# A two-layer spectral and convolution kernel: halves of the array in turn, pole planes loaded first, a second bank for the last batch

## The chip, the cores and the metric

The kernel runs on one core of one Trainium2 chip. A core has a matrix engine (TensorE, PE in the profile; PEld is its weight loading), a vector engine (VectorE, DVE), a scalar engine (ScalarE, ACT), a general engine (GpSimd, POOL) and an engine that only issues transfers here (SyncE, SP). Each runs its own instructions in their order, and they meet through semaphores. Transfers between device memory and the on-chip memory (SBUF) run on 16 DMA engines; SP and POOL each issue into a queue of their own. TensorE writes to PSUM, an accumulation memory[...]. The metric is the device time of the core, in microseconds (us).

## The reference

Input x is 16 batches x 16 channels x 256 x 256, float32. Two layers, each of the form x = x + layer(group_norm(x)), with 8 groups of 2 channels:

```
# layer 0: a Fourier layer with poles
alpha = fft2(gn(x))
A  = 1 / (omega1 - pole1);  Bm = 1 / (omega2 - pole2)      # 4 poles per axis and channel pair
S  = einsum('ikpq,oikp,xikq->oxik', residue, A, Bm)
out1 = einsum('biox,oxik->bkox', alpha, S)                 # mix of channels i -> k per frequency
out2 = einsum('bikpq,ikpq->bkpq', einsum(alpha, A, Bm), residue)
x = x + real(ifft2(out1)) + real(out2 x exponentials) / (256 * 256)

# layer 1: convolutions and a gate
f = mish(conv3x3(gn(x) per channel, 1 -> 4 features));  top, bot = halves of f's rows
ker = conv1x1(relu(conv1x1(bot)));  ti = sum over 9 taps of patches(top) * ker
out = mish(conv3x3(concat(ti, roll(bot)), 64 -> 16))
gate = sigmoid(3-tap conv over channels of mean(out));  x = x + gn(x) * gate
```

## The kernel before, in words

The kernel is four functions that run one after the other: `layer0_forward`, `layer0_mix`, `layer0_back` and `layer1`. What passes between them lies in device memory: `al` (spectrum), `hd` (mixed spectrum), `zn` (normalized input of layer 1), `cf` (features of layer 1), and tables `td`, `avd`, `ed`. In the forward the order of TensorE's instructions is the one written in the source, and a scheduler orders the other engines. In the other three functions PE, ACT, DVE and POOL all keep the order of the source. SP's transfers are ordered by the scheduler throughout. A tile pool with `bufs=n` gives n buffers to a tag in turn; a writer waits until the readers of the buffer's last tile are done.

**Forward.** 64 steps, one for each batch b and group of four channels (cg). A step loads x one step or two ahead (`fetch`, L162), computes the group norm's scalars with two tiny matmuls (gn_mean L34, gn_var L42) and DVE work between them (gnq L36 to L39), and forms the even and odd halves `eo`. `rows` multiplies by the Fourier table along y (pu, L207) and by the pole table (pv, L214), twice a step; ACT copies `right` (L222), DVE combines into `u` (L224), ACT writes `v` (L231). `poles` then computes `pd` (L241): for each of 2 pairs j of channels and 2 channels a of a pair, four accumulating products with 64 output columns, written to partitions 64a to 64a+63, so that channel a uses one half of the array. In the steps of every batch but the first, `columns` multiplies the batch before by the Fourier table along x (px, L313): for two frequency rows k of a tile, two halves h and two parts accumulate; row k is written to partitions 64k to 64k+63, again one half of the array. ACT moves px to `o` (L320), and POOL stores it to `al` (L329). The pool of px has two buffers. From step 4 on, DVE also computes tables, a piece a step (L415 to L534, L767 to L781). After the last step, `finish` and nine calls of `columns` do the last batch.

**Mix.** 33 groups g of four frequencies along y. `poles` (L618) multiplies the pole planes `av`, a 192 KB load of a group (L617), by a mask m8 into `lt` (L627, six DVE instructions); `residues` (L636) multiplies lt by the table `tt` into `s`: for each k, part v and half h one product to partitions 64h to 64h+63 (L641); DVE and ACT copy the products (L649, L651). `spread` copies the loaded spectrum `alc` into the operand `alb` (L598 on ACT, L600 on DVE). `mix` then multiplies s and alb (pg, L663), `turn` transposes, and `columns` transforms along x. Before the loop, SP's order is: ident, ix (1 MB), m8, four loads of tt (1 MB each), m4, eight loads of alc, then av of groups 0 and 1.

**Back** transforms along y, adds the poles' part and the input, and writes zn; the change doesn't touch it.

**Layer 1.** Units of rows (9 a batch) pass conv1 (L1027), mish (L1046, L1075), the reduction (L1054) and the involution (L1095, L1103, L1106), whose results go to cf. One batch behind, `conv2` (L1153) reads 17 row pairs for each of eight steps s (`rows`, L1155, 2176 KB, two buffers) and computes two halves q, each 24 accumulating products of 32 columns into one bank (c2ps, L1169), which ACT reads with mish and a running sum (e, L1178). c2ps has a pool of one bank (ps2); the pool psd with three banks serves the reduction, the involution and the gate's product. After a batch, `gate` (L1182) reduces the sums, forms a scale per channel, and in eight parts (four channels of half the rows) loads zn into `o` (L1193, four buffers), applies scale and mean on POOL (four instructions, L1216) and stores to the output (L1225). For the last batch no units are left: conv2's eight steps run alone, with the gate of the batch before beside them, and then its own gate ends the kernel.

Of the kernel before, what the change touches and what calls it, by code (L numbers as in the profile page):

```python
# [19 lines left out]
N = 256  # L20
G = 8
P = 128
# [50 lines left out]
def layer0_forward(ctx, tc, d, al, bd, tabs):  # L73
# [160 lines left out]
    def poles(cg, vts, acc):  # L234

        pd = psd.tile([P, 2, P], F32, tag="pd", name="pd")
        for j, vt in enumerate(vts):
            for a in range(2):
                ch = 4 * cg + 2 * j + a
                for n, (xh, k) in enumerate(((0, 0), (0, 1), (1, 0), (1, 1))):  # L240
                    nc.tensor.matmul(  # L241
                        pd[64 * a : 64 * a + 64, j],
                        lhsT=vt[:, a, xh, 64 * k : 64 * k + 64],
                        rhs=bt[:, xh, ch, 1 - k : 3 - k].rearrange("p l m -> p (l m)"),
                        start=n == 0,
                        stop=n == 3,
                    )
        gs = slice(2 * cg, 2 * cg + 2)

        def times(out, part, coef):  # L250
            shape = [P, 2, part.shape[2] // M, M]
            nc.vector.tensor_tensor(
                out.rearrange("p g (k q) -> p g k q", q=M),
                part.rearrange("p g (k q) -> p g k q", q=M),
                coef[:, gs].unsqueeze(2).to_broadcast(shape),
                ALU.mult,
            )

        t = dp.tile([P, 2, P], F32, tag="t", name="t")
# [42 lines left out]
    def columns(b, g0, rsc):  # L302

        u = us[b % 2]
        n = min(4, NF - g0)
        o = op.tile([P, 2, 2, N], F32, tag="o", name="o")
        for j in range(0, n, 2):
            lanes = 64 * min(2, n - j)
            ps = psx.tile([P, 2, 2, H], F32, tag="px", name="px")
            for k in range(min(2, n - j)):  # L310
                for h in range(2):
                    for part in range(2):
                        nc.tensor.matmul(  # L313
                            ps[64 * k : 64 * k + 64, :, h],
                            lhsT=u[:, h, part, g0 + j + k].rearrange("p f c -> p (f c)"),
                            rhs=wxn[:, h, part],
                            start=part == 0,
                            stop=part == 1,
                        )
            nc.scalar.activation(  # L320
                o[:lanes, j // 2],
                ps[:lanes].rearrange("p v h x -> p v (h x)"),
                AF.Copy,
                scale=rsc[:lanes],
            )
        for k in range(min(2, n)):
            w = (n - k + 1) // 2
            for v in range(2):
                nc.gpsimd.dma_start(  # L329
                    out=al[g0 + k : g0 + n : 2, v, :, b].rearrange("g p x -> p g x"),  # L330
                    in_=o[64 * k : 64 * k + 64, :w, v],
                )
# [221 lines left out]
def layer0_mix(ctx, tc, d, al, hd, tabs):  # L554
# [3 lines left out]
    nc = tc.nc  # L558
    nb = d["x"].shape[0]
    cp = ctx.enter_context(tc.tile_pool(name="mc", bufs=1))  # L560
    ident = load(nc, cp, d["ident"], [P, P], "ident")
    ix = load(nc, cp, d["ix"], [P, 8, N], "ix")
    m8 = load(nc, cp, d["m8"], [P, 8], "m8")

    tt = cp.tile([P, 2, C, N], F32, name="tt")
    for k in range(0, C, 4):
        nc.sync.dma_start(out=tt[:, :, k : k + 4], in_=tabs[0][:, :, k : k + 4])
    avd = tabs[1]

    alb = cp.tile([P, N, 4, nb], F32, name="alb")
    m4 = load(nc, cp, d["m4"], [P, 4], "m4")

    ap = ctx.enter_context(tc.tile_pool(name="ma", bufs=2))
    lp = ctx.enter_context(tc.tile_pool(name="ml", bufs=1))
    gp = ctx.enter_context(tc.tile_pool(name="mg", bufs=1))
    hp = ctx.enter_context(tc.tile_pool(name="mh", bufs=3))
# [31 lines left out]
    def spread(spectrum, f):  # L610
        for eng, parts in zip((nc.scalar, nc.vector), spreads[f]):
            for q, j in parts:
                expand(spectrum[q], q, j, eng)

    def load_poles(g):
        av = ap.tile([P, 32, 4, 3], F32, tag="av", name="av")
        nc.sync.dma_start(out=av.rearrange("p k f l -> p (k f l)"), in_=avd[g])  # L617
        return av  # L618

    def poles(av):  # L620

# [101 lines left out]
    E = mybir.EngineType  # L723
    with tc.manual_schedule(engines={E.PE, E.Activation, E.DVE, E.Pool}):
        spectrum = [load_spectrum(0, q) for q in range(4)]
        lt = poles(load_poles(0))
        av = load_poles(1)
        s = gp.tile([P, N, 2, C], F32, tag="s", name="s")
        for k0 in range(0, C, 2):
# [201 lines left out]
def layer1(ctx, tc, d, zn, cf, mr, nb):  # L931
# [225 lines left out]
    def conv2(b, s, acc):  # L1157
# [3 lines left out]

        begin = ((H + 1, 1, H + 2), (0, H + 1, 1))
        for q in range(2):
            ps = ps2.tile([P, 4, H], F32, tag="c2", name="c2ps")
            for blk in range(2):
                for dx in range(3):
                    x = begin[q][dx]
# [13 lines left out]
    def gate(b, acc):  # L1181
# [29 lines left out]
        for k in range(0, 8, 2):  # L1211
            following = [part(k + 2), part(k + 3)] if k < 6 else None
            c = k // 2 * 4
            for half, o in enumerate(parts):
                for i in range(4):
                    nc.gpsimd.tensor_scalar(  # L1216
                        o[:, i],
                        o[:, i],
                        scale[:, c + i : c + i + 1],
# [275 lines left out]
```

## Time and profile before

| what | value |
|---|---|
| median of 3 runs | 7388.45 us (7382.54 to 7390.2) |
| the profiled execution | 7392.98 us |
| its span, first to last instruction | 7391.2 us |
| PE busy | 6831.1 us (92%) |
| DVE busy | 4961.8 us (67%) |
| ACT busy | 3806.5 us (51%) |
| POOL busy | 3475.6 us (47%) |
| px, L313 | x4224, 557.8 us busy, 385 ns mean |
| pd, L241 | x2048, 164.3 us busy, 279 ns mean |
| c2ps, L1169 | x12288, 1395.3 us busy, 601 ns mean |
| gate's o, L1216 on POOL | x512, 280.5 us busy, 555 ns mean |

A profile is of one execution, taken on the chip. "Busy" is the time in which at least one instruction of a group runs; matmuls overlap, so busy time over count is less than the mean duration. The ends of matmuls are modelled. A fp32 matmul leaves two records, each with its weight load. In a timeline, a row merges instructions of one kind that follow each other: start, length, engine, line, operation, output<-input, partitions x elements, count, and in brackets the idle time before and what ended it. The forward runs from 0 to about 1408 us, the mix to about 2968, the back to about 3611, layer 1 to the end.

### The profile page before, as it was taken

The numbers are of one execution on the slowest core, as the hardware profiler recorded it, in microseconds if no ns is written. First come the engines' busy times: TensorE is split into PE (matmuls) and PEld (weight loads), VectorE is DVE, ScalarE is ACT, GpSimd is POOL, SyncE is SP. The second block draws the span as 40 slices with busy tenths as digits, with TensorE's granted clock in tenths as the row PEclk, the third lists the DMA queues.
The fourth block names the chain that finished last, engine by engine and source line by source line (L and its number), as shares of the span: only waits on it lengthen the run. The fifth ranks groups of instructions, "written<-read, shape, count | busy, mean of one in ns | idle before, by whom it ended". The sixth has DMA issues, their size and how long they took to land.

```text
span 7391.2 us, 147380 instructions
## 1 busy us (share of the span) xinstructions
PE 6831.1 (92%) x57640; PEld 3890.3 (53%) x57640; DVE 4961.8 (67%) x9441; ACT 3806.5 (51%) x5915; POOL 3475.6 (47%) x4636
## 2 busy tenths in 40 slices
PE   7889999799999999899789999999999999999996
PEld 5778888566666666677423333333333333333332
DVE  8999975366666666788676656665666666666662
ACT  2223333366666666222366656666666666656662
POOL 2334444322222222566554655555665565655554
PEclk9899999899999999999889999999999999999999
DMA  3444444333333332899767888888888888888886
GB/s 99 111 117 119 118 124 117 109 95 97 98 98 98 98 98 83 305 326 326 249 181 221 259 242 253 252 258 254 253 253 251 256 249 267 256 247 251 256 265 205
DMA packets 716089, 1443.59 MB, mean 195 GB/s; under 512 B 98954, under 2 KB 525254, under 8 KB 673638
## 3 DMA queue, kind: packets, MB, share of 16 engines
q1 hardware_dynamic: 567206, 959.76, 43.4%
q0 software_dynamic: 148192, 474.40, 20.6%
q8 instruction: 460, 7.54, 0.4%
q14 instruction: 231, 1.89, 0.1%
HBM read 877.12 MB, written 556.47 MB: 194 GB/s over the span
## 4 chain that ended last, share of the span: by engine, by line
PE 64%; DVE 7%; ACT 4%; issue 3%; DMA 2%; POOL 0%; SPq 0%; DVEq 0%; ACTq 0%; POOLq 0%
PE c2ps L1169 17%; PE c L1027 12%; PE pd L1095 12%; PE ph L698 5%; PE ps L641 5%; PE pg L663 4%; ACT wide L1075 3%; DVE alb L600 2%; PE pr L1054 2%; PE py L858 2%; PE py L859 2%; PE pt L679 1%; DVE zb L890 1%; DVE st L875 1%; DMA rows<-cf 1%
## 5 line engine op out<-in xcount | busy, mean ns | idle before, releaser
L1075 ACT ACTIVATE wide<-c,b 32x512 f32<-32x512 f32 x2176 | 1477.4, 679 | 354.6 <-PE c L1027 302.8
L1103 DVE TENSOR_TENSOR t<-pd,r 64x512 f32<-64x512 f32 x1088 | 744.3, 684 | 1295.9 <-PE pd L1095 1270.3
L1106 DVE TENSOR_TENSOR top<-pd,t 32x512 f32<-32x512 f32 x2176 | 1504.2, 691 | 52.6
L1169 PE MATMUL c2ps<-rows,c 128*32 128x512 f32 x12288 | 1395.3, 601 | 26.6 <-ACT e L1178 13.7
L1087 POOL COPY wide<-wide 32x1031 f32<-32x1031 f32 (+1 forms) x576 | 568.9, 988 | 1239.0 <-ACT wide L1075 1211.7
L1027 PE MATMUL c<-z,w 102*128 102x512 f32 x2048 | 1014.2, 628 | 138.5 <-ACT wide L1075 115.4
L1095 PE MATMUL pd<-wide,dw 128*128 128x512 f32 x2048 | 1012.5, 616 | 6.4 <-ACT r L1063 2.5
L1169 PEld LDWEIGHTS c2ps<-rows,c 128*32 128x32 f32 x12288 | 393.0, 109 | 993.6 <-issue 885.3
L718 POOL DMA_DIRECT2D hd<-h x512 | 323.5, 639 | 1227.6 <-DVE h L711 1203.5
L1027 PEld LDWEIGHTS c<-z,w 102*128 102x128 f32 x2048 | 401.2, 198 | 675.9 <-issue 486.0
L1095 PEld LDWEIGHTS pd<-wide,dw 128*128 128x128 f32 x2048 | 376.8, 194 | 614.3 <-issue 449.0
L1178 ACT ACTIVATE e<-c2ps,b 128x512 f32<-128x512 f32 x256 | 175.9, 687 | 845.6 <-PE c2ps L1169 842.9
L1088 POOL COPY wide<-wide 32x1031 f32<-32x1031 f32 (+1 forms) x576 | 572.2, 993 | 35.8
L313 PE MATMUL px<-wxn,u 128*64 128x256 f32 x4224 | 557.8, 385 | 2.2 <-ACT o L320 2.1
L641 PE MATMUL ps<-tt,lt 128*64 128x256 f32 x4224 | 495.5, 384 | 38.9 <-DVE lt L627 35.9
L698 PE MATMUL ph<-ix,yt 64*128 64x256 f32 x4128 | 502.5, 391 | 5.4 <-issue 4.7
L313 PEld LDWEIGHTS px<-wxn,u 128*64 128x64 f32 x4224 | 400.7, 136 | 127.0 <-ACT o L320 5.1
L698 PEld LDWEIGHTS ph<-ix,yt 64*128 64x128 f32 x4128 | 392.7, 190 | 91.7 <-issue 44.6
L1046 ACT ACTIVATE bot<-c,b 128x512 f32<-128x512 f32 x544 | 344.1, 684 | 175.7 <-PE c L1027 168.2
L207 PE MATMUL pu<-fy,eo 128*128 128x128 f32 x2048 | 425.5, 291 | 6.0 <-DVE u L224 4.4
L320 ACT ACTIVATE o<-px,rsc 128x512 f32<-128x512 f32 (+1 forms) x272 | 186.0, 686 | 472.2 <-PE px L313 441.1
L871 POOL TENSOR_TENSOR x<-x,o 128x512 f32<-128x512 f32 x256 | 324.0, 1266 | 216.7 <-DVE o L870 215.3
(203 smaller groups left out, 10818.5 us busy)
## 6 DMA issues: line engine op xcount, KB each, us to landing
rows<-cf SPq DMA_DIRECT2D x128, 2176.0 KB
z<-zn SPq DMA_DIRECT2D x768, 257.8 KB
cf<-top POOLq DMA_DIRECT2D x512, 240.0 KB, 7.1
cf<-bot POOLq DMA_DIRECT2D x96, 840.0 KB, 11.6
alc<-al SPq DMA_DIRECT2D x264, 256.0 KB
zn<-zb SPq DMA_DIRECT2D x128, 516.0 KB
o<-zn SPq DMA_DIRECT2D x128, 516.0 KB
z<-in_x SPq DMA_DIRECT2D x64, 1024.0 KB
```

The lines of the kernel that those rows point to most:

```text
L207: nc.tensor.matmul(pu[:, xh, e].rearrange("p v m -> p (v m)"), lhsT=lhs, rhs=fy[:, e], start=True, stop=True,)
L313: nc.tensor.matmul(ps[64 * k : 64 * k + 64, :, h], lhsT=u[:, h, part, g0 + j + k].rearrange("p f c -> p (f c)"), rhs=wxn[:, h, part], star ...
L641: nc.tensor.matmul(ps[64 * h : 64 * h + 64, v], lhsT=lt[:, h, k, 1 - v : 3 - v].rearrange("p l f c -> p (l f c)"), rhs=tt[:, h, k], start= ...
L698: nc.tensor.matmul(ph[q][:, e], lhsT=yt[lanes, i].rearrange("p t k -> p (t k)"), rhs=ix[lanes, i], start=n == 0, stop=n == 3,)
L1027: nc.tensor.matmul(ps[:, a], lhsT=w, rhs=z[:k, c : c + 2, 0:N], start=True, stop=True)
L1075: nc.scalar.activation(self.feat[64 - 32 * q : 96 - 32 * q, f, self.groups[g], :H], ps[q][32 * f : 32 * f + 32], AF.Mish, bias=b1[0][32 * ...
L1087: nc.gpsimd.tensor_copy(flat[0:32, f, 1:m], flat[64:96, f, 0 : m - 1])
L1088: nc.gpsimd.tensor_copy(flat[96:128, f, 0 : m - 1], flat[32:64, f, 1:m])
L1095: nc.tensor.matmul(ps, lhsT=dwt if self.tail else dw, rhs=self.feat[:, f, cs, :H], start=True, stop=True,)
L1103: nc.vector.tensor_tensor(t[64:128], ps[:64], self.r[:, cs], ALU.mult)
L1106: nc.vector.tensor_tensor(self.top[32 * f : 32 * f + 32, cs, q], ps[lanes], t[lanes], ALU.add)
L1169: nc.tensor.matmul(ps[32 * j : 32 * j + 32], lhsT=c2[:, blk, dx, :], rhs=t[:, 4 * j + blk : 4 * j + blk + 4, x : x + H], start=(blk, dx) = ...
```

## The change

Four edits. In the forward, `poles` issues the four accumulating products of two channels in turn, channel 0 and channel 1 alternating, instead of four of one and then four of the other; `columns` does the same with the two frequency rows k. The number of products and the tiles stay. In the mix, `load_poles` is defined earlier and the planes of group 0 are loaded right behind m8, ahead of tt; ident and ix follow tt. In layer 1, the second half q of every conv2 step of the last batch writes to a bank of psd instead of ps2. In the gate of the last batch, three of the four scaling instructions of a part go to DVE. Apart from these, each engine's instructions stand in the same order as before.

```diff
@@ layer0_forward.poles
         for j, vt in enumerate(vts):
-            for a in range(2):
-                ch = 4 * cg + 2 * j + a
-                for n, (xh, k) in enumerate(((0, 0), (0, 1), (1, 0), (1, 1))):
+            for n, (xh, k) in enumerate(((0, 0), (0, 1), (1, 0), (1, 1))):
+                for a in range(2):
+                    ch = 4 * cg + 2 * j + a
                     nc.tensor.matmul(
                         pd[64 * a : 64 * a + 64, j],
@@ layer0_forward.columns
-            for k in range(min(2, n - j)):
-                for h in range(2):
-                    for part in range(2):
+            for h in range(2):
+                for part in range(2):
+                    for k in range(min(2, n - j)):
                         nc.tensor.matmul(
                             ps[64 * k : 64 * k + 64, :, h],
@@ layer0_mix
-    ident = load(nc, cp, d["ident"], [P, P], "ident")
-    ix = load(nc, cp, d["ix"], [P, 8, N], "ix")
     m8 = load(nc, cp, d["m8"], [P, 8], "m8")
+    ap = ctx.enter_context(tc.tile_pool(name="ma", bufs=2))
+    avd = tabs[1]
+
+    def load_poles(g):
+        av = ap.tile([P, 32, 4, 3], F32, tag="av", name="av")
+        nc.sync.dma_start(out=av.rearrange("p k f l -> p (k f l)"), in_=avd[g])
+        return av
+
+    av = load_poles(0)
 
     tt = cp.tile([P, 2, C, N], F32, name="tt")
     for k in range(0, C, 4):
         nc.sync.dma_start(out=tt[:, :, k : k + 4], in_=tabs[0][:, :, k : k + 4])
-    avd = tabs[1]
+    ident = load(nc, cp, d["ident"], [P, P], "ident")
+    ix = load(nc, cp, d["ix"], [P, 8, N], "ix")
...
-        lt = poles(load_poles(0))
+        lt = poles(av)
         av = load_poles(1)
@@ layer1.conv2
         for q in range(2):
-            ps = ps2.tile([P, 4, H], F32, tag="c2", name="c2ps")
+
+            pool, tag = (psd, "d") if q and b == nb - 1 else (ps2, "c2")
+            ps = pool.tile([P, 4, H], F32, tag=tag, name="c2ps")
@@ layer1.gate
                 for i in range(4):
-                    nc.gpsimd.tensor_scalar(
+                    eng = nc.vector if i and b == nb - 1 else nc.gpsimd
+                    eng.tensor_scalar(
                         o[:, i],
                         o[:, i],
```

More of the change, by code (lines that the diff above doesn't have):

```diff
@@ L567, in layer0_mix @@
         nc.sync.dma_start(out=tt[:, :, k : k + 4], in_=tabs[0][:, :, k : k + 4])
-    avd = tabs[1]
+    ident = load(nc, cp, d["ident"], [P, P], "ident")
+    ix = load(nc, cp, d["ix"], [P, 8, N], "ix")
     alb = cp.tile([P, N, 4, nb], F32, name="alb")
     m4 = load(nc, cp, d["m4"], [P, 4], "m4")
-    ap = ctx.enter_context(tc.tile_pool(name="ma", bufs=2))
     lp = ctx.enter_context(tc.tile_pool(name="ml", bufs=1))
@@ L613, in spread @@
                 expand(spectrum[q], q, j, eng)
[L615 to L618, printed above, removed]
     def poles(av):
```

## The prediction

> **What bounds the kernel now.** I read the page first, then busy time by stretch, then waits and timelines of the places that the diff touches. The page's two rows, 185 us a slice:
>
> ```profile
> span 7391.2 us, 147380 instructions
> ...
> PE   7889999799999999899789999999999999999996
> ...
> DVE  8999975366666666788676656665666666666662
> ```
>
> TensorE (PE) is full nearly everywhere, so work taken off it should show, except in the first slices, where the vector engine (DVE) is as full. The forward stage ends at 1408 us (last px matmul). It has 64 steps, one per batch and channel group; a step runs from one start of pd to the next. Busy time in three stretches of it (columns: stretch, length, then busy us and count of PE, PEld, DVE, ACT, POOL; granted clock; DMA share; GB/s):
>
> ```profile
> 167.20:552.40 385.20, 338.65 (x2662) 296.15 (x2661) 353.90 (x1050) 104.82 (x194) 138.79 (x189) 0.91 0.41 113
> 552.40:1049.60 497.20, 490.51 (x4394) 422.59 (x4393) 457.43 (x1167) 188.53 (x333) 236.58 (x323) 1.00 0.45 122
> 1049.60:1362.90 313.30, 313.30 (x2866) 272.82 (x2865) 162.49 (x499) 96.25 (x191) 149.48 (x211) 1.00 0.40 105
> ```
>
> These are steps 5 to 19, 20 to 45 and 46 to 62. In the last, PE has no gap and DVE is half idle: PE alone binds. In the first, DVE builds tables and PE waits for it: the waits of that stretch give `PE gn_var L42 <- DVE gnq L39` 44.5 us in 15 waits, 3 us a step. The middle is shared. Its DVE waits:
>
> ```profile
> DVE arg L525 <- ACT n L523: 11.9, 12, 2.0
> DVE gnq L36 <- PE gn_mean L34: 9.6, 14, 1.6
> DVE arg L515 <- DMA ed<-arg: 6.5, 6, 1.5
> DVE st L174 <- DMA z<-in_x: 4.5, 6, 1.4
> ```
>
> One PE-bound step in the timeline (start, length, then what), and residue products of the mix, which already take the halves in turn:
>
> ```profile
> 1105.40 2.24 PE L241 MATMUL pd<-bt,v 128*64 128x128 f32 x29
> 1107.38 0.43 PE L313 MATMUL px<-wxn,u 128*64 128x256 f32 x1
> ...
> 1107.86 7.90 PE L313 MATMUL px<-wxn,u 128*64 128x256 f32 x62
> 1115.69 0.38 PE L34 MATMUL gn_mean<-mv,ones 128*128 128x2 f32 x2
> ```
>
> ```profile
> 2002.32 3.67 PE L641 MATMUL ps<-tt,lt 128*64 128x256 f32 x32
> 2005.92 0.92 PE L698 MATMUL ph<-ix,yt 64*128 64x256 f32 x6
> ```
>
> An fp32 matmul leaves two records. Forward: 32 pd and 64 px records take 1115.69 - 1105.40 = 10.29 us. Mix: 32 records of px's shape take 2005.92 - 2002.32 = 3.60 us, 112 ns each with the start; record starts inside are 216 ns apart per half, 108 overall. px also overlaps already (its starts come 920 ns per 8 records, 115 each, in mid-run, because a half's run of four overlaps the other's), but each burst begins and ends with one half alone.
>
> The mix's start:
>
> ```profile
> 1409.56 3.72 SPq L567 DMA_DIRECT2D tt<-td  x4
> ...
> 1430.80 14.40 SPq L617 DMA_DIRECT2D av<-avd  x3
> 1441.15 3.70 DVE L627 TENSOR_TENSOR lt<-av,m 128x512 f32<-128x512 f32 x6 [66.15 <-DMA av<-avd]
> ...
> 1444.91 5.43 PE L641 MATMUL ps<-tt,lt 128*64 128x256 f32 x34 [0.68 <-DVE lt L627]
> ```
>
> PE stands from 1408 to 1443 for 192 KB of pole planes that are queued behind 4 MB of tt, 1 MB of ix and 2 MB of alc. The end of layer 1:
>
> ```profile
> 7297.55 5.40 PE L1169 MATMUL c2ps<-rows,c 128*32 128x512 f32 x48 [0.95 <-ACT e L1178]
> ...
> 7317.70 5.44 PE L1169 MATMUL c2ps<-rows,c 128*32 128x512 f32 x48 [1.95 <-DMA rows<-cf]
> ```
>
> Each conv2 half waits some 0.95 us for ACT to empty the one bank; two of the later ones wait for rows instead.
>
> **What the Trainium skill says.** TensorEngine Tiling (Array Packing), Key Properties: "Different tiles can execute LdWeights and Matmul in parallel"; the 3.60 us above agree. TensorE: Matmul & The Clock Gate, Part 1: an idle window of some 3.4 us halves the PE clock; the mean of 0.91 where PE waits, 1.00 elsewhere, agrees. DMA: Bandwidth & Descriptors, Queues, rings and completion order: descriptors of one ring are taken in order; av, issued at 1430.80 behind alc and used at 1441.15, agrees. SBUF — State Buffer, Who interferes with whom: DVE's two-port tensor_scalar and GpSimd (POOL) block each other; no row of this trace shows it for the new tail.
>
> **Part 1, forward (pd and px by halves in turn).** Nothing is added; the same 96 records per step, in the same place of every queue. pd: full-width 128-column records start 109 ns apart (8 transposes pt take 1.09 us), so two halves in turn 54.5: 32 x 54.5 = 1.74. px: 64 x 108 = 6.91. Start 0.15 as in the mix. Sum 8.80 against 10.29: 1.49 saved a step (1.54 in one step of four, which has 8 px records more). A px tile then takes 1.73 us instead of 1.84; ACT empties it in 0.69 behind two buffers, so no new wait. By stretch:
> - steps 0 to 3, pd alone: some 0.5 each, 2.0. Step 4 (PE full in it): 1.5.
> - steps 5 to 19: PE's saved time is added to its 3 us wait for gnq, which stands behind table work on DVE. DVE's own waits there (24.6 us, u on right) follow gn_var and not px. 0.
> - steps 20 to 45: from below 0, from above 497.2 - 457.4 = 39.8 by DVE's busy time, or 26 x 1.49 = 38.7. DVE's waits for the sine on ACT (11.9) and for DMAs (6.5 + 4.5) are only partly PE's doing; if they stay, 457.4 + 22.9 = 480.3, 17 saved. I take 17.
> - steps 46 to 62: 17 x 1.49 = 25.3.
> - the last 9 columns: ACT's o also waits for al's stores there; 0.5 of a possible 2.
> Sum 46, bounds 29 and 68.
>
> **Part 2, pole planes first.** The same loads, in another order: 192 KB of av ahead of tt, ident and ix (1.06 MB) behind it, m8 first. SP's queue starts as before, at 1408.0, when px ends. av then lands near 1412; lt takes 3.7 us from 1413.4 (ACT's last o ends at 1413.3, and lt waits for ACT), done at 1417.1. tt's first MB: ix, in its place before, ran from 1410.1 to 1416.0 beside al's stores, so tt's first quarter lands near 1417 and the others 2.5 us apart (4 MB in 10 us before). Residues need a quarter per 3.5 us, so they start at 1417 and keep going. Before they had lt complete at 1444.9, less 1 us for the four records ahead of it: 27 earlier. What is late next: ix and alc move 5 MB as before and still end near 1440; the copies of alc into alb begin at 1434 instead of 1461 and take q by q 2.9 us, q3 at 1442: just covered. The second av, behind alc, lands near 1441 and is needed at 1446. The first pg starts at 1473.35 - 27 = 1446. If alc is 5 us later, 22 is left; bounds 22 and 28.
>
> **Part 3, second bank for the last batch's conv2.** 16 halves end 6.38 us apart (ACT e) and hold 48 records x 108 = 5.2; one bank more takes away 1.17 each, at most 18. The borrowed bank is free: the last pd starts at 7250.3. But rows must come: 2.2 MB a step s, read in SP's order with the previous gate's o loads between. In 7278 to 7304 the DMA share is 0.99; rows of s=2 were landed only at 7276.5, used at 7277.85; rows of s=5 are issued at 7306.19, after o loads that wait for stores of POOL's gate, which is no faster now, and landed at 7316.9. So s=5 starts at about 7316.2 instead of 7317.7 (1.5 saved), and only its six halves more count in full: 5 x 1.17 = 5.9. Sum 7.4, bounds 5 and 18.
>
> **Part 4, three of four gate operations on DVE in the last batch.** Now POOL takes 4 x 0.55 + 0.3 + 0.79 = 3.3 us a part, eight parts, 7358.38 to the last store's issue at 7384.10, landed at 7387.5. After: 0.55 on POOL beside 3 x 0.34 on DVE (the 128x256 tensor_scalar row, 342 ns; if the port makes them take turns, 1.6 in sum), then 1.1 for the issue: 1.7 to 2.7 a part. Then DMA binds: 8 stores (1.45 us each alone) and 4 loads (2.05) are 20 us, and loads of parts 4 to 7 wait 3.4 us for stores of parts 0 to 3. I follow them to a last landing 24.5 after the start, against 29: 5 saved, bounds 2 and 10.
>
> Sum: 46 + 27 + 7.4 + 5 = 85. The profiled execution took 7392.98 (1.8 around its span): 7308; the runs' median 7388.45 is 4.5 below it: 7303.
>
> **Rivals.**
> 1. DVE takes over (steps 20 to 45 give 0, more idle PE lowers its clock). For: DVE is busy 92% there. Against: 9.6 us of its waits are for PE's gn_mean. Gain 29 + 27 + 12 = 68: 7320.
> 2. Nothing else binds: steps 20 to 45 give 38, rows are early, DMA keeps up in the tail: 68 + 27 + 28 = 123, 7265. Against: the 0.99 DMA share.
> 3. Part 1 doesn't do what it says, since px overlaps already (115 against 108): 39 left, 7349. Against: burst ends and pd, counted above.
> 4. Slower: a half's load (137 ns) is no longer hidden when the other half's record comes between, so px records cost (216 + 137) / 2 = 176 instead of 130 in 44 steps: +130, net +91, 7479. It decides from about 144 a record. Against: L641, same shape, 108.
>
> **Chances.** Forecast 0.62; rival 1 0.17; rival 2 0.12; rival 3 0.06; rival 4 0.03. The range 7272 to 7328 takes in the forecast with its bounds, rival 1 and half of rival 2. 0.2% (15 us) is about what a measurement tells from no change. Faster 0.96, same 0.01, slower 0.03.
>
> **What would show it.** Right: pd to gn_mean 8.8 us in late steps; steps 5 to 19 as long as now, with longer waits for gnq; first pg near 38 us after px's end instead of 65; waits of c2ps for ACT gone but for rows present; DMA share near 1 in the last 25 us. Wrong: late steps near 10.3, alb waiting for alc by more than 5 us, s=5 starting on ACT and not on rows.

## The result, and the profile after

The changed kernel takes 7315.62 us (median of 4 runs, 7312.28 to 7327.95) against 7385.49 us for the kernel before, measured beside it: a ratio of 0.9912, 95% interval 0.9893 to 0.993, so 52 to 79 us faster. The prediction was 7303 in a range of 7272 to 7328. The profiled execution took 7312.28 us. Its page, the rows that answer to those shown of before, and the groups of px and pu (busy us and mean ns of one, then idle time ahead and what ended it):

```profile
span 7310.5 us, 147410 instructions
...
PE   7889999899999998999789999999999999999997
...
DVE  8999975466666665888666666666666666666662
...
L313 PE MATMUL px<-wxn,u 128*64 128x256 f32 x4224 | 481.9, 379 | 8.0 <-ACT o L320 7.9
L207 PE MATMUL pu<-fy,eo 128*128 128x128 f32 x2048 | 426.8, 292 | 26.8 <-DVE u L224 21.8
```

px fell from 557.8 to 481.9 us busy, 76 less, yet the forward stage ended only 33.7 us earlier. The last line says where to look: pu, the first product of the next step, now waits 21.8 us for DVE's u (4.4 before).

**Where the time went.** The two traces, cut at the same events (a record's end for "last", its start for "first"; the rows sum to the spans):

| stretch, us | before | after | difference | predicted |
|---|---|---|---|---|
| start to last px | 1407.97 | 1374.24 | -33.7 | -46 |
| last px to first pg | 65.38 | 39.27 | -26.1 | -27 |
| mix, first pg to first pf | 1500.86 | 1497.33 | -3.5 | 0 |
| first pf to first c | 666.08 | 665.71 | -0.4 | 0 |
| layer 1, first to last c | 3592.04 | 3585.11 | -6.9 | 0 |
| last c to last c2ps | 122.73 | 117.27 | -5.5 | -7.4 |
| last c2ps to the end | 36.15 | 31.58 | -4.6 | -5 |

The four stretches that the change touches give 69.9 us. The other 10.8 lie in code that it doesn't touch; the single-part runs below show that differences of this size are scatter between executions.

**Forward.** The three stretches of steps 5 to 19, 20 to 45 and 46 to 62 (columns as in the prediction):

```profile
163.90:548.30 384.40, 321.18 (x2663) 270.04 (x2662) 353.07 (x1050) 104.98 (x194) 138.31 (x189) 0.90 0.40 114
548.30:1040.10 491.80, 457.87 (x4395) 377.06 (x4394) 454.73 (x1167) 188.59 (x333) 237.14 (x323) 0.99 0.46 123
1040.10:1332.60 292.50, 292.50 (x2865) 242.74 (x2864) 162.32 (x499) 96.30 (x191) 149.86 (x211) 1.00 0.42 113
```

PE's busy time fell in all three, by 17.5, 32.6 and 20.8 us; the lengths fell by 0.8, 5.4 and 20.8. In the first PE's wait for gnq rose from 44.5 to 59.2 us, as predicted (us in total, times, longest):

```profile
PE gn_var L42 <- DVE gnq L39: 59.2, 15, 5.3
```

In the middle stretch DVE's busy time is nearly what it was (457.4 then, 454.7 now), and so is its idle time (39.8 then, 37.1 now). Most of PE's gain turned into waits. PE's longest there, then DVE's:

```profile
PE pu L207 <- DVE u L224: 19.2, 14, 1.9
PE px L313 <- ACT o L320: 7.2, 4, 1.9
PE gn_var L42 <- DVE gnq L39: 3.4, 6, 0.9
```

```profile
DVE arg L515 <- DMA ed<-arg: 17.0, 7, 3.6
DVE arg L525 <- ACT n L523: 10.5, 12, 1.8
DVE st L174 <- DMA z<-in_x: 2.2, 4, 1.2
```

A clean step, PE's timeline (start, length, what):

```profile
1092.48 2.04 PE L241 MATMUL pd<-bt,v 128*64 128x128 f32 x32
1094.35 7.08 PE L313 MATMUL px<-wxn,u 128*64 128x256 f32 x64
1101.35 0.38 PE L34 MATMUL gn_mean<-mv,ones 128*128 128x2 f32 x2
```

pd to gn_mean takes 8.87 us against 10.29. pd's 32 records are now one group with none of px among them. But one step in four, with 72 px records:

```profile
1125.80 2.04 PE L241 MATMUL pd<-bt,v 128*64 128x128 f32 x32
1127.67 8.80 PE L313 MATMUL px<-wxn,u 128*64 128x256 f32 x72
1136.40 0.38 PE L34 MATMUL gn_mean<-mv,ones 128*128 128x2 f32 x2
```

This is 10.60 us. The same step of the kernel before, its pd, the bulk of its px and the end:

```profile
1141.55 2.24 PE L241 MATMUL pd<-bt,v 128*64 128x128 f32 x29
...
1144.01 8.82 PE L313 MATMUL px<-wxn,u 128*64 128x256 f32 x70
1152.76 0.38 PE L34 MATMUL gn_mean<-mv,ones 128*128 128x2 f32 x2
```

11.21 us. It gained 0.61, not the 1.54 of the prediction: the eight extra px records cost 10.60 - 8.87 = 1.73 us now, 216 ns each, and 11.21 - 10.29 = 0.92 before.

**Mix's start** (transfers are SP's issues; in brackets the idle time before and what ended it):

```profile
1374.95 0.34 SPq L567 DMA_DIRECT2D av<-avd  x1
1375.34 2.61 SPq L574 DMA_DIRECT2D tt<-td  x4
1378.05 3.70 DVE L629 TENSOR_TENSOR lt<-av,m 128x512 f32<-128x512 f32 x6 [33.93 <-DMA av<-avd]
1384.24 16.40 PE L643 MATMUL ps<-tt,lt 128*64 128x256 f32 x128 [10.00 <-DMA tt<-td]
1400.65 11.04 ACT L605 ACTIVATE alb<-alc,m 128x1024 f32<-128x1024 f32 x6
1401.55 11.76 DVE L607 TENSOR_SCALAR alb<-alc,m 128x1024 f32<-128x1024 f32 x10
1413.52 4.81 PE L665 MATMUL pg<-alb,s 128*32 128x64 f32 x233 [12.87 <-issue]
```

PE stands 10.0 us for tt's first quarter (9 predicted), all 128 residue records run in one go, and then the copies of alc set the first pg. They start 26.4 us behind px's end (26 predicted); DVE's end at 1413.31, and pg starts 0.2 us later, 39.3 us behind px's end (38 predicted).

**The end.** conv2 of the last batch has no wait for ACT left; what it waits for is rows. The 16 halves of 48 records run in four rows of the timeline, three of which follow a wait (the first, s = 0 and 1, started at 7179.37):

```profile
7206.00 11.93 PE L1173 MATMUL c2ps<-rows,c 128*32 128x512 f32 x96 [5.58 <-DMA rows<-cf]
7219.66 21.05 PE L1173 MATMUL c2ps<-rows,c 128*32 128x512 f32 x192 [1.72 <-DMA rows<-cf]
7245.29 33.65 PE L1173 MATMUL c2ps<-rows,c 128*32 128x512 f32 x288 [4.58 <-DMA rows<-cf]
```

And the last gate, its first DVE and POOL work, the loads of parts 4 to 7 and the first of them to be used:

```profile
7282.26 0.56 POOL L1221 TENSOR_SCALAR o<-o,scale,mean 128x258 f32<-128x258 f32 x1 [54.68 <-DVE scale L1213]
7282.37 4.81 DVE L1221 TENSOR_SCALAR o<-o,scale,mean 128x258 f32<-128x258 f32 x12 [0.23 <-DVE scale L1213]
...
7287.69 9.11 SPq L1197 DMA_DIRECT2D o<-zn  x4
...
7291.88 1.18 DVE L1221 TENSOR_SCALAR o<-o,scale,mean 128x258 f32<-128x258 f32 x3 [4.70 <-DMA o<-zn]
```

The first four parts are done in 1.7 to 1.9 us each; then the loads of the others, which wait for the stores of these, take over the pace. DMA's share in the last 25 us is 0.72.

### The profile page after: what moved, and what is told of

Same layout as the page of the kernel before. It is cut to its first block, busy times and chain, and to the rows that moved or that the text cites. A ratio compares the mean times of both kernels' runs of the same rounds, so it can differ in the third digit from the quotient of the medians.

```text
span 7310.5 us, 147410 instructions
## 1 busy us (share of the span) xinstructions
PE 6750.3 (92%) x57640; PEld 3787.1 (52%) x57640; DVE 4970.2 (68%) x9465; ACT 3811.4 (52%) x5915; POOL 3470.0 (47%) x4612
## 4 chain that ended last, share of the span: by engine, by line
PE 71%; DVE 16%; DMA 4%; ACT 4%; issue 3%; POOL 1%; SPq 0%; DVEq 0%; ACTq 0%; POOLq 0%
PE c2ps L1173 18%; PE c L1029 12%; PE pd L1097 12%; PE ph L700 5%; PE ps L643 5%; PE pg L665 4%; PE px L313 3%; ACT wide L1077 3%; DVE alb L607 2%; PE pu L207 2%; PE pr L1056 2%; PE py L860 2%; PE pv L214 2%; PE py L861 2%; DVE u L224 2%
## 5 line engine op out<-in xcount | busy, mean ns | idle before, releaser
L313 PE MATMUL px<-wxn,u 128*64 128x256 f32 x4224 | 481.9, 379 | 8.0 <-ACT o L320 7.9
L207 PE MATMUL pu<-fy,eo 128*128 128x128 f32 x2048 | 426.8, 292 | 26.8 <-DVE u L224 21.8
L607 DVE TENSOR_SCALAR alb<-alc,m 128x1024 f32<-128x1024 f32 x330 | 419.9, 1396 | 0.0
L214 PE MATMUL pv<-at,eo 128*128 128x128 f32 x2048 | 413.3, 285 | 0.0
```

Source lines behind the costliest of these rows:

```text
L207: nc.tensor.matmul(pu[:, xh, e].rearrange("p v m -> p (v m)"), lhsT=lhs, rhs=fy[:, e], start=True, stop=True,)
L313: nc.tensor.matmul(ps[64 * k : 64 * k + 64, :, h], lhsT=u[:, h, part, g0 + j + k].rearrange("p f c -> p (f c)"), rhs=wxn[:, h, part], star ...
```

## Experiments

### Each part alone

Four kernels, each the kernel before with one part of the diff: `x1_forward` the two loop orders, `x2_poles` the load order of the mix, `x3_bank` the line `pool, tag = (psd, "d") if q and b == nb - 1 else (ps2, "c2")`, `x4_gate` the line `eng = nc.vector if i and b == nb - 1 else nc.gpsimd`.

> The kernel before with the forward products by halves in turn (part 1) alone. My theory: the last px ends some 34 us earlier than in the kernel before, as in the changed kernel: some 21 us in steps 46 to 62, 5 in steps 20 to 45, under 1 in steps 5 to 19, and nothing is given back later, so the total falls by 34 (about 7354). Rival: the forward stage's gain needs the other parts, or what comes behind it absorbs a part (the pole planes come at a fixed time, say): then the first pg comes less than 30 us earlier. The mix from the first pg to the first pf, and layer 1 from first to last c, are untouched: if they too change by 3 and 7 us as in the changed kernel, then part 1 does that by some way I have not seen; if not, that is scatter between executions.

> The kernel before with the mix's pole planes first (part 2) alone. My theory: from px's end to the first pg 65.7 us fall to about 39.6, so the total falls by 26 (about 7362), and px ends at 1408 as before. Rival: a part of the 26 is due to the earlier forward stage, and it is less than 23 alone. The mix behind it and layer 1 unchanged within 1 us if what the changed kernel showed there (3.5 and 6.9 less) is scatter.

> The kernel before with conv2's second bank in the last batch (part 3) alone. My theory: from the last c record to the last c2ps record 117.3 us as in the changed kernel, against 122.7: the waits for ACT are gone, and waits for rows of 12 us in sum take the place of what they gave. Rival: without the other parts the loads come otherwise, and it is under 3 or over 8 us.

> The kernel before with three of four operations of the last gate on DVE (part 4) alone. My theory: from the last total to the end 35.2 us fall to 30.6 as in the changed kernel, because the stores' pace by POOL gives way to loads waiting for stores. Rival: part 3 had a share in it, and alone it is under 3.

Measured: part 1 alone 7359.87 us against 7387.28 before (ratio 0.9961, 0.9946 to 0.9976); part 2 alone 7363.02 (0.9969, 0.9957 to 0.998). Of parts 3 and 4 there is one run each. The stretches of the profiled executions:

| us | before | part 1 | part 2 | part 3 | part 4 | all |
|---|---|---|---|---|---|---|
| start to last px | 1407.97 | 1377.82 | 1404.38 | 1407.16 | 1404.47 | 1374.24 |
| last px to first pg | 65.38 | 64.62 | 40.06 | 68.08 | 64.52 | 39.27 |
| mix | 1500.86 | 1508.00 | 1497.60 | 1492.24 | 1503.03 | 1497.33 |
| layer 1, first to last c | 3592.04 | 3582.00 | 3588.41 | 3597.18 | 3592.52 | 3585.11 |
| last c to last c2ps | 122.73 | 122.08 | 121.94 | 116.27 | 121.85 | 117.27 |
| last c2ps to the end | 36.15 | 37.65 | 36.67 | 36.27 | 31.68 | 31.58 |

Each part moves its own stretch, and what differs elsewhere is no more than kernels with the same code there differ by. So the parts add: 30.2 + 25.3 + 6.5 + 4.5 = 66.5. The forward scatters too: with its code unchanged it ended at 1404.4 to 1408.0 us, so some 3 us of the 33.7 of the result may be scatter. The mix differs by 16 us and layer 1 by 15 among kernels that have the same code there. That is the scatter that the 3.5 and 6.9 us of the result belong to. Part 1's total fell by 27 and not by the 34 expected; with an interval of 18 to 40 us the two don't contradict each other. (The expectations count the tail from the last total, 1 us behind the last c2ps.)

The steps of the forward, from one start of pd to another:

| us | before | part 1 alone | all parts | predicted |
|---|---|---|---|---|
| to the first pd | 103.58 | 103.26 | 102.58 | 0 |
| steps 0 to 4 | 63.58 | 61.37 | 61.29 | -3.5 |
| steps 5 to 19 | 385.22 | 385.03 | 384.41 | 0 |
| steps 20 to 45 | 497.19 | 493.91 | 491.78 | -17 |
| steps 46 to 62 | 313.32 | 292.54 | 292.55 | -25.3 |
| step 63 and the last columns | 45.10 | 41.73 | 41.64 | -0.5 |

### Is it DVE that took the gain of steps 20 to 45?

First, the six polynomial terms are left out of the exponential, in the kernel before and in the changed one.

```diff
     nc.vector.tensor_scalar(n, y, 1 / 5040, None, ALU.mult)
-    for c in (1 / 720, 1 / 120, 1 / 24, 1 / 6, 1 / 2, 1.0):
-        nc.vector.scalar_tensor_tensor(n, n, c, y, ALU.add, ALU.mult)
```

> The kernel before, with the six polynomial terms of the exponential left out (16 tables, 96 operations of 0.69 us on DVE, 13 of the tables in steps 20 to 45), so the spectra are not the reference's; everything else stands. It is the base for the next run. Theory (DVE bounds steps 20 to 45): these steps fall from 497 us to what PE needs, 20 clean steps of 18.07 and 6 of 19.71, that is 480. Rival (other waits than DVE hold them): they stay over 490.

> The changed kernel with the same six terms left out. Theory (DVE ate part 1's gain in steps 20 to 45): with DVE's 54 us gone, these steps take 20 x 16.66 + 6 x 19.10 = 448 to 455 us, so part 1 is worth 25 to 32 there instead of 5.4, against the run just before. Rival (it is PE's own products or a wait for a load that eats it): they stay over 480 and part 1 is worth under 10. Steps 5 to 19 hold 3 of the tables, 12 us of DVE: by the theory they fall by about 12 in both runs and part 1 stays worth under 2 there.

Measured: steps 20 to 45 took 496.7 us in the first and 485.8 in the second, steps 5 to 19 took 382.9 and 384.6. The theory's numbers (480; 448 to 455; 12 less in the steps ahead) all missed. The rival's "over 490" and "over 480" came, but part 1 was worth 10.9 and not under 10. Cutting the stretch shows why:

| us | before | after | cut before | cut after |
|---|---|---|---|---|
| steps 20 to 36 | 325.7 | 319.7 | 330.8 | 331.0 |
| steps 37 to 45 | 171.4 | 172.0 | 165.9 | 154.8 |

The scheduler, which orders DVE's instructions in the forward, pulled the tables together: no table operation is left behind step 36. The gap that the cut was to make in DVE's work was filled with later tables, so DVE was not relieved in steps 20 to 36, and there part 1 is worth -0.2 us between the cut kernels. In the nine steps behind, with no table, it is worth 11.1: seven clean steps at 1.41 and two long ones at 0.61 make 11.1. The cut stretch, steps 20 to 36 (but for their last 1.6 us) and 37 to 45 of the cut changed kernel; DVE is busy for 90% of the first part and 59% of the second:

```profile
550.40:879.80 329.40, 305.56 (x2864) 253.06 (x2864) 297.59 (x778) 134.51 (x228) 155.19 (x211) 0.97 0.45 123
881.40:1036.20 154.80, 154.80 (x1517) 128.57 (x1516) 91.35 (x282) 50.96 (x102) 80.15 (x112) 1.00 0.46 126
```

This speaks for DVE but isn't what was forecast, so a second kernel takes the tables themselves away: the body of the table's loop under `if not k:`, one sine and exponential per axis instead of eight, stored eight times.

> The changed kernel with each axis's exponential and sine computed for the first two poles alone and stored eight times, so 14 of 16 such tables (each some 13 to 15 us of DVE) are left out and the poles' part of the output is not the reference's; loads, stores and products stand. The run that left six terms out did not free DVE where I wanted: its order of work changed and the tables closed up to step 36. Here nearly all of that work is gone from steps 20 to 45. Theory (DVE alone took part 1's gain there): these steps take what PE needs, 20 x 16.66 + 6 x 19.10 = 448 us, 455 at most, against 480 that the kernel before could reach with no DVE work at all; and steps 5 to 19 stay near 384, since their tables are others. Rival (ACT, a bank of px, or x's loads hold these steps): over 470.

Measured: steps 20 to 45 took 450.1 us, inside the 448 to 455 of the theory; steps 5 to 19 took 379.1 where "near 384" was expected, since one of the three tables that the changed kernel computes there is gone; but another kernel with the changed kernel's own forward (the rows experiment below) took 380.7, so much of the 5.3 us less may be scatter. The span was 7279.2 us.

```profile
543.70:993.90 450.20, 449.93 (x4395) 373.37 (x4394) 263.78 (x812) 148.10 (x294) 231.97 (x323) 1.00 0.47 128
```

PE is busy for 449.93 of 450.20 us, and it has no wait in this stretch. So it was the work on the tables that had held PE there: neither x's loads nor px's banks take its place. What this kernel can't tell apart is DVE's part of that work from ACT's: with the tables went DVE's operations and its waits for ed's stores, but also the sines on ACT and 28 of the 32 ACT_TABLE_LOADs (1.28 us each) from step 4 on. The last experiment below tells them apart.

### The lone row

The 33 frequency rows of a batch end with a single one (`n - j == 1`); its products use one half of the array, and since part 1 nothing runs on the other half meanwhile. This kernel puts its two halves h on the array's two halves:

```diff
+            if n - j == 1:
+                for part in range(2):
+                    for h in range(2):
+                        nc.tensor.matmul(
+                            ps[64 * h : 64 * h + 64, :, h],
+                            lhsT=u[:, h, part, g0 + j].rearrange("p f c -> p (f c)"),
...
+                for h in range(2):
+                    half = slice(64 * h, 64 * h + 64)
+                    nc.scalar.activation(
+                        o[:64, j // 2, :, H * h : H * h + H],
+                        ps[half, :, h],
+                        AF.Copy,
+                        scale=rsc[half],
+                    )
+                continue
```

> The changed kernel, but where a group of columns ends with one lone row (one step in four), its two halves h are put on the array's two halves in turn and emptied by two ACT copies of 64x256. My reading: the 8 records of the lone row stand alone on one half at 216 ns each, 1.72 us, and so the step of 72 px records gained 0.61 us and not 1.54. Then they take some 0.86 us here: the long steps of 46 to 62 fall from 19.09 to about 18.23 us, and the stretch by 4 x 0.86 = 3.4; steps 20 to 45 by 0 to 5, the last columns by 0 to 1; the end of px 3.5 to 9 us earlier. Rival: the extra 0.86 is the wait for a px bank or for ACT's copy, and the long steps stay above 18.9, or grow by the second copy.

Measured: a long step of 46 to 62 takes 18.24 us, 0.86 less, as expected:

```profile
1147.35 7.08 PE L332 MATMUL px<-wxn,u 128*64 128x256 f32 x64
1154.26 1.03 PE L313 MATMUL px<-wxn,u 128*64 128x256 f32 x8
1155.22 0.39 PE L34 MATMUL gn_mean<-mv,ones 128*128 128x2 f32 x2
```

The eight records take 0.96 us where they took 1.73. But the end of px came 16 us later, not earlier: steps 5 to 19 took 373.9 us (10.5 less than in the changed kernel) and steps 20 to 45 took 521.8, 30 more. PE's and DVE's waits in the latter (DVE's from 548 us on):

```profile
PE pu L207 <- DVE u L224: 32.2, 20, 2.4
PE gn_var L42 <- DVE gnq L39: 8.0, 9, 1.5
```

```profile
DVE arg L534 <- DMA ed<-arg: 19.7, 6, 4.1
DVE u L224 <- ACT right L222: 18.7, 21, 1.7
DVE n L536 <- DMA ed<-n: 12.9, 5, 3.7
```

The built programs differ in more than the edit: with one more ACT instruction in every such step the scheduler orders DVE's work anew; in the traces the two orders part at the 486th of 9465 DVE instructions. In the new one DVE waits 32.6 us for stores of its tables (17.0 in the changed kernel's stretch) and 18.7 for ACT's right (1.1). The test of that reading keeps DVE's order: the split for batches 10 on alone (`if n - j == 1 and b >= 10`), where no table is computed any more. DVE's instructions then stand as in the changed kernel, but for a few that start within 0.02 us of each other. The same run has eight buffers for the gate's parts (below).

> The changed kernel with eight buffers for the gate's parts, and with the lone row's halves in turn, but only for batches 10 on (steps 47, 51, 55, 59 and the last columns), where no table is computed any more; the order of DVE's instructions is then the changed kernel's own, which it was not in the run that split every lone row. Theory (that run lost its 30 us in steps 20 to 45 through the scheduler's new order of DVE, not through the split): steps 20 to 45 stay at 490 to 493; steps 46 to 62 take 292.5 - 4 x 0.86 = 289.1, the last columns 0.9 less, the tail 22.9. Together 11 us below the changed kernel: about 7304. Rival (the second copy or its waits cost time wherever it stands): steps 46 to 62 not below 291.

Measured: steps 20 to 45 took 491.2 us, steps 46 to 62 took 289.4 (3.2 less), step 63 and the last columns 40.8 (0.9 less). So the split is worth what was expected where DVE has no tables, and the 30 us came with the order. The first of the two kernels says so as well: in steps 20 to 45 its six long steps, which hold the split, took 112.3 us against 128.9 in the changed kernel, and its twenty others 409.5 against 362.9. Which exchange in the order costs them was not singled out.

### Rows of the last batch

```diff
-        nc.sync.dma_start(out=t[:, :, 1 : N + 1], in_=flat[:, 16 * s : 16 * s + 17])
+        eng = nc.scalar if b == nb - 1 and s > 1 else nc.sync
+        eng.dma_start(out=t[:, :, 1 : N + 1], in_=flat[:, 16 * s : 16 * s + 17])
```

> The changed kernel with the last batch's rows of steps s = 2 to 7 issued by ACT and not by SP. My theory: rows are late because they stand in SP's queue behind the gate's loads o, which wait for buffers that POOL's gate frees; then the waits of c2ps for rows (5.6 + 1.7 + 4.6 = 11.9 us) go to under 4 and the time from the last c to the last c2ps falls from 117.3 to about 109, what 16 halves of 24 products need being 16 x 5.2 = 83 and the rest lying before and between. Rival: the transfers are bound by the memory (DMA share 0.99), so rows come as late from any queue: the waits stay above 9, and the time above 115. A third way: ACT issues a transfer only behind its mish of the half before, which can make rows late by itself; then the waits stand at other steps.

Measured: from last c to last c2ps 114.5 us, 2.7 less, and 11.1 us of waits for rows against 11.9:

```profile
7213.30 12.32 PE L1174 MATMUL c2ps<-rows,c 128*32 128x512 f32 x96 [4.25 <-DMA rows<-cf]
7229.50 10.62 PE L1174 MATMUL c2ps<-rows,c 128*32 128x512 f32 x96 [3.88 <-DMA rows<-cf]
7243.09 41.74 PE L1174 MATMUL c2ps<-rows,c 128*32 128x512 f32 x384 [2.97 <-DMA rows<-cf]
```

The theory's 109 and the rival's "above 115" were both missed. The queue is not what binds: ACT's issues at 7199.13, 7213.75 and 7225.80 are used 14 to 17 us later, while 2176 KB at this stretch's 363 GB/s would be 6.1. The first and third of them went out within 0.5 us of the end of the half that frees their buffer (7198.65, 7225.62) and came as late. In 7213 to 7244 this kernel's DMA share is 1.01; the changed kernel's is 0.98 in 7206 to 7246. The bytes of rows, the gate's loads and its stores bind there. The third way of the expectation had a share too: the issue of s = 3 stood 4.7 us on ACT (its buffer was free at 7209.05), and the waits now stand at s = 2, 3 and 4 instead of 2, 3 and 5. Where do the 2.7 us come from, then? 0.8 is shorter waits, and most of the rest the clock. The last halves of the two kernels, the changed one first:

```profile
7245.30:7279.00 33.70, 33.64 (x288) 11.72 (x288) 0.00 (x0) 3.90 (x10) 0.00 (x0) 0.93 0.36 113
```

```profile
7243.00:7285.00 42.00, 41.74 (x384) 19.47 (x384) 0.00 (x0) 5.51 (x15) 0.00 (x0) 1.00 0.49 158
```

A record takes 116.8 ns at a granted clock of 0.93 and 108.7 ns at 1.00: 2.3 us over 288 records. In the changed kernel the stretch follows a wait of 4.58 us, in this one a wait of 2.97. At s = 2 it is the other way, by 0.4 us (12.32 us for 96 records here, 11.93 there). The clock differs between executions, too: five kernels with the same conv2 code and four buffers took 115.8 to 117.3 us from last c to last c2ps, so the 114.5 is barely outside their scatter.

### The gate's parts

```diff
-    op = ctx.enter_context(tc.tile_pool(name="l1o", bufs=4))
+    op = ctx.enter_context(tc.tile_pool(name="l1o", bufs=8))
```

> The changed kernel with eight buffers for the gate's parts in place of four. My theory of the tail: loads of parts 4 to 7 wait 4.70, 3.09, 1.66 and 1.35 us for the stores of parts 0 to 3; with a buffer of its own each part's load goes out at once, and from the last total to the end 30.6 us fall by 6 to 10, to about 22. Rival: the 12 transfers' bytes bound the tail (DMA share near 1 after the first parts): it falls by under 3. Beside it, the gates of the other batches get eight buffers too: the waits of c2ps for rows may shrink, since loads o then stand less in SP's queue; conv2 of the last batch falls by 0 to 8 for that.

Measured: from the last c2ps to the end 24.8 us against 31.6, 6.8 less; span 7300.0. No load is left in the tail; DVE works without a gap, and POOL, an operation and a store's issue a part, sets the pace at 1.7 to 1.9 us:

```profile
7278.51 0.55 POOL L1221 TENSOR_SCALAR o<-o,scale,mean 128x258 f32<-128x258 f32 x1 [61.92 <-DVE scale L1213]
7278.56 9.35 DVE L1221 TENSOR_SCALAR o<-o,scale,mean 128x258 f32<-128x258 f32 x24 [0.16 <-DVE scale L1213]
```

conv2 of the last batch took 115.7 us, 1.5 less, which is inside the scatter just named. Together with the late lone rows (the run above) this makes 7295.14 us, a ratio to before of 0.9878 (0.9861 to 0.9894), 9 below the 7304 expected: layer 1 from first to last c took 3578.6 us instead of 3585.1, on which see the last section.

### Taking DVE's load off

DVE's work on the tables can be done by another engine without leaving anything out. The kernel just above (late lone rows, eight buffers), and in `exponential`:

```diff
     nc.vector.tensor_scalar(y, y, -88.0, 88.8, ALU.max, ALU.min)
-    nc.vector.tensor_scalar(n, y, float(1 / np.log(2)), ROUND, ALU.mult, ALU.add)
...
-    nc.vector.scalar_tensor_tensor(y, n, 1.0, bits.bitcast(F32), ALU.add, ALU.mult)
+    nc.scalar.activation(y, y, AF.Exp)
```

> The run before, with the exponential of the tables by ACT's Exp in place of 13 of its 14 operations on DVE, so that nothing is left out: 16 tables x some 9.8 us leave DVE, ACT gets 16 activations of 0.6 and a table load of 1.28 us or two each. Theory (DVE is what holds steps 20 to 45 after the change): these steps fall from 492 to 448 to 465, as when the tables were computed once (450), and the total by 27 to 44 more, to about 7268. Rival (ACT, with table loads in front of the copies that PE waits for, takes DVE's place; or DVE's new order costs as much as in the run that split every lone row): over 480, and the total is not below 7295.

Measured: 7251.47 us (7249.31 to 7258.67), a ratio to before of 0.982 (0.9806 to 0.9835), against 0.9878 without this edit, measured beside it. Steps 20 to 45 took 460.8 us, steps 5 to 19 took 376.4 (8 less).

```profile
540.60:1001.40 460.80, 451.70 (x4394) 373.77 (x4392) 315.95 (x940) 196.43 (x344) 233.66 (x323) 1.00 0.47 129
```

DVE's share of the stretch fell from 92 to 69%, PE's rose from 93 to 98%; ACT carries 8 us more. So it was DVE's part of the table work, and not ACT's, that held PE. The scheduler pulled the tables together here too: the last one stands in step 29. The sixteen steps behind it took 277.1 us, PE's own need (12 x 16.66 + 4 x 19.10 = 276); the ten with tables took 183.7, still 10 more than in the kernel without tables (173.5). This kernel is faster than both before and after.

## Why the prediction was right, and where it was off

The time fell inside the range, and each part moved its own stretch as its step said, part 1 by less than told. The forecast's sum of 85 us was 15 too high, though: the touched stretches gave 69.9, which is nearer to rival 1's sum (68, "DVE takes over") than to the forecast's. By the steps:

- **Steps 0 to 4, 3.5.** 2.3 (2.2 with part 1 alone): a third less than told.
- **Clean step, 1.49 saved.** 1.41 measured, pd 1.87 and px 7.00 against the 1.74 + 0.15 and 6.91 of the sum. Right, for 13 of the 17 steps.
- **"1.54 in one step of four".** Wrong: 0.61. The step priced the extra eight records as if they alternated; a lone row has no partner. Before, its run of eight overlapped the end of the run ahead (0.92 us), and part 1 took that overlap away (1.73). The sum's 17 x 1.49 lacks 4 x 0.88 = 3.5 us for it, of the 4.5 missing in steps 46 to 62; the split of the lone row gave it back at 0.86 a step.
- **Steps 5 to 19 at 0.** Right (0.2 alone, 0.8 with all), with the longer wait for gnq that it named.
- **Steps 20 to 45, "I take 17".** The failed step, and the largest part of the 15. It kept 22.9 us of DVE's waits and let the other 17 of its idle time go as PE got faster. They didn't go: DVE was idle for 39.8 us before and for 37.1 after. Its waits for gnq's mean (9.6) went, but its wait for ed's stores rose from 6.5 to 17.0, and PE's for u from 3.7 to 19.2. 5.4 measured, 3.3 with part 1 alone; four kernels with the changed forward took 490.9 to 494.6 us here, four with the old one 497.2 to 497.8, so the gain is 3 to 7. Why the stores of ed are waited for longer stays open. Rival 1 was right about this place: with the tables gone the stretch took 450 us, PE's own need, and with Exp on ACT 461. Its other half, a lower clock, hardly came: 0.99 against 1.00.
- **The last columns, 0.5 of a possible 2.** 3.4. Step 63 was in no line of the sum. It and the nine columns together gained more than was taken for the columns.
- **Mix's start, 27.** 26.1, and 25.3 alone: residues wait for tt, then the copies of alc set the first pg, as told. The Trainium skill's statement that one ring takes its descriptors in order (DMA: Bandwidth & Descriptors, Queues, rings and completion order) is what this step rested on; the trace agrees: av, now issued at 1374.95 ahead of tt, was used at 1378.05, and tt only at 1384.24.
- **Second bank, 7.4.** 5.5. Rows gate s = 5 as told: its start, counted from the last c, came 1.7 us earlier (1.5 predicted). The mis-sized term is "only its six halves more count in full: 5 x 1.17": they gained 3.7 and not 5.9, because a half took 5.6 us in the mean and not 5.2, at a granted clock of 0.93 where before had 1.00. All of it lies in the first of the six, which took 7.4 us: the granted clock is 0.50 in the 4.5 us behind the wait and 1.00 from there on, and the other five took 5.2 each. The skill (TensorE: Matmul & The Clock Gate, Part 1) lets an idle PE lose its clock, and the trace agrees: the wait ahead of the six halves had grown from 1.95 to 4.58 us. (The landings of rows that the sum uses, 7276.5 and 7316.9, are 7276.99 and 7317.56 by the trace's semaphores; the step does not depend on that.)
- **Gate tail, 5.** 4.6, with the loads waiting for stores as told (4.70, 3.09, 1.66 and 1.35 us). But "then DMA binds", with a share near 1 in the last 25 us as its sign, did not come: the share was 0.72. What held the tail was that each load stood behind a store; with eight buffers no load is left in the tail, and it fell by another 6.8 us.
- **Rivals 2, 3 and 4.** Nothing else binding (7265) fell in steps 20 to 45 and at conv2's rows. Part 1 does what it says. No weight load came to light: px records stand 108 ns apart.

How near the total came is partly luck. The two profiled executions differ by 80.7 us, of which 10.8 is scatter in code that the change doesn't touch; the medians differ by 69.9, the same as the touched stretches, which is chance to the digit when executions of the kernel before run from 7371 to 7397 us. The 4.5 us between median and profile that the forecast carried over are scatter of the same kind.

## What to carry to other kernels

Where a profile shows an engine 92% busy beside the one that is relieved, don't count the busy engine's idle time as room: here it had 39.8 us of it before the change and 37.1 after, and the gain was 5 and not 17. Relieving that engine as well was worth 44 us, 39 of them in the forward of the profiled executions, where the whole change had brought 70. When work is put in pairs, look for the item without a partner: it loses the overlap that it had by chance (the lone row's 0.92 us became 1.73 here). And where a scheduler orders the work, compare the orders of all engines before reading a small edit's time, since one more ACT instruction in every fourth step came with 30 us here.

## What the runs showed of the hardware

- Two halves of the array overlap even when four products of one half follow four of the other, at 115 ns a record against 108 in turn; a half alone runs at 216 ns. The gain of taking turns is small in the middle of a burst, and a single-half tail costs double.
- TensorE does not start everything in the order of its program, as the first section has it of every engine. In the step that the prediction shows of the kernel before, the first px record starts at 1107.38 us while three of pd's 32, which stand ahead of it in the program, are still to start (the last at 1107.70): a product on one half passes earlier ones on the other. With the halves in turn pd's 32 records stand together.
- Waits of PE of some 4 us cost clock, but not by their length alone. Ahead of conv2's stretches in the last batch of three kernels (changed, rows on ACT, eight buffers), behind those of 3.74, 4.17, 4.25, 4.58 and 5.58 us the granted clock was 0.50 for up to 5.6 us and the stretch 1.4 to 2.7 us too long; behind those of 0.58, 1.72, 2.97 and 3.88 us it was 1.00.
- In the gate DVE's operation takes 0.40 us and POOL's 0.56 where neither overlaps the other's. Where they overlap, two things are seen in the changed kernel: an operation of DVE that lasts 0.75 us and ends 0.15 us behind POOL's, which keeps its 0.57 (7284.96 to 7285.72 and 7285.00 to 7285.56), or POOL's stretched to 0.73 beside one of DVE's of 0.58. The skill (SBUF — State Buffer, Who interferes with whom) calls the port that they share in DVE's two-port modes an exclusive lock (which mode DVE was in, no run here shows); the first kind agrees with DVE waiting POOL's operation out, the second costs both some 0.17 us. Either way a part took 1.7 to 1.9 us, inside the 1.7 to 2.7 of the prediction.
- Eight buffers for the gate's parts also shortened layer 1 ahead of the last batch: first to last c took 3578.3 to 3579.1 us in the three kernels that have them, 3582.0 to 3597.2 in the eleven that don't. The traces show why: in this stretch conv2 waits 3.7 to 13.0 us for rows in the eleven and never in the three, as the expectation of the run with eight buffers had it. The waits go with the lengths (3.7 us in the shortest of the eleven, 13.0 in the longest), so they account for much of layer 1's scatter in the tables above.
